# Two-layer attention and recurrence: order of the denominators' sums, and later slots for some projections

## The chip, the cores and the metric

The kernel runs on one NeuronCore of a Trainium2 chip. The metric is the device time of one execution in microseconds. Before the change three runs took 2109.12, 2111.13 and 2114.09 us (median 2111.13).

## What is computed

The input `x` has four batches of 128 channels and 64 x 64 positions, so N = 4096 positions (tokens) per batch, in float32. Two layers follow each other:

```python
# layer 0: attention over all positions, 64 inner channels
att = softmax(einsum('bmi,bmj->bij', wk @ x, wq @ x), axis=2)
x   = x + wo @ (att applied to wv @ x)

# layer 1: token layout t = x^T
t = t + causal_attention(_ln_t(t), Wq, Wk, Wv)        # 128 channels, scale 128**-0.5
t = t + ffn(_ln_t(t), W, V, gamma, beta)
# ffn: Wx = batchnorm(_ln_t(t) @ W^T), then over time
#      y_t = sigmoid(Wx_t + y_{t-1} @ V^T)
```

## The kernel before

`fast_path` does the work (another path, taken when a range flag is set, did not run). All of `x` stays in SBUF as `xs`. A batch has NB = 8 blocks of 512 query positions per layer. The kernel runs batch by batch: the eight blocks of layer 0, then the eight of layer 1.

**Items and slots.** Each block is cut into items of two key tiles (128 keys each) against the 512 queries: 16 items for a block of layer 0, 2g + 2 items for block g of the causal layer 1. The main loop (L923) gives every item a slot `s`. In slot `s` TensorE forms the scores of item `s` (`scores`, L791 in layer 0, L800 in layer 1) into PSUM `s_ps` (two buffers), ScalarE takes the exponential into `p` (L805, L807; four buffers), VectorE (DVE) adds `p` into `dsum` (`sums`, L831 and L839), and TensorE multiplies the `p` of item `s - 2` with the values into `acc` (`values`, L851 and L859). A `p` buffer is free again when both the values and the sum have read it.

**Block's end.** With the last item of a block, `values` copies `acc` to SBUF (`half` L870 and the add L871 in layer 0, `agg` L873 in layer 1), and DVE adds the two halves of `dsum` into `den` (L875). What remains for the block is a chain of small tasks, which the loop runs in later slots, one due task per slot at most, the earliest due first; slots without one go to the `side` list (the next batch's keys and values).

- `folded` (L561) sums `den` over partitions: a 32 x 32 block transpose (L565) and a reduction (L567) leave `part`, four quarters per token. Either TensorE sums and spreads them (`by_pe`, L573, with a DVE multiply L574), or five DMAs on the SP queue carry them through DRAM (four L579, then L580). The result is `own`.
- `project` (L583) sums the quarters of `own` (L586), inverts the sum (L587), multiplies `agg` with the output matrix in four matmuls into `o_ps` (L590) and adds the scaled result to `xs` in four DVE instructions (L595, called STTs below).
- `normed` (L599) is the layer norm of the block: statistics, a power on GpSimd (POOL, L458), a few short DVE steps (L459 to L462) and four scalings (L611).
- Layer 0 continues with `by_channels` (L655): a DVE transpose and eight SP DMAs (L659, L664) that form `xhT`. Layer 1 (`finish1`, L683) writes the block to `x2` (L701), forms its own `xhT` with a DVE transpose and five SP DMAs (`second`, L719 and L723), and multiplies it with the recurrence's input matrix (`third`, L727), with statistics on DVE (L730) and a copy into `xs` on ScalarE (L740).

In layer 0 the projection is not tied to a slot: `first` (L672) folds and puts `second` on the list `fill`, and the main loop takes one entry from `fill` at the end of the next block (L938). In layer 1 the numbers of `yield` (L750 to L756) say how many slots after the task before a task is due: `first` two slots after `sums`, `second` three after `first`, `third` four after `second` (six for the blocks folded on TensorE, g < 2).

**Who sets the order.** Slots give the order in which instructions are written. The tile framework then orders each engine's queue by a simulated time of its own, with the written order as priority, so an instruction whose inputs it takes to be ready may be put ahead of others written earlier. `tc.keep_in_program_order(ins)` adds an edge from the instruction last written for the same engine to `ins`; it is an order in the queue and no semaphore. After the last block the recurrence over time and the output follow.

Of the kernel before, what the change touches and what calls it, by code (L numbers as in the profile page):

```python
# [11 lines left out]
ALU = mybir.AluOpType  # L12
AX = mybir.AxisListType
# [336 lines left out]
def fast_path(  # L350
# [21 lines left out]
    nc = tc.nc  # L372
# [4 lines left out]
    NB = N // BLK  # L377
# [86 lines left out]
    with tc.tile_pool(name="batch", bufs=1) as batch, tc.tile_pool(name="rows", bufs=2) as rowp, tc.tile_pool(  # L464
# [7 lines left out]
        def misc(name):  # L472
            return ps_m.tile([P, BLK], F32, tag="m", name=name)
# [109 lines left out]
        def project(layer, b, g, agg, own):  # L583

            rec = recs[:, layer, b, ts(g, TPB)]
            nc.vector.tensor_reduce(rec, own.rearrange("p q j -> p j q"), AX.X, ALU.add)  # L586
            nc.vector.reciprocal(rec, rec)  # L587
            op = misc("o_ps")
            for j in range(TPB):
                nc.tensor.matmul(  # L590
                    op[:, ts(j, P)], lhsT=agg[:, ts(j, P)], rhs=wv1 if layer else wo2, start=True, stop=True
                )
            for j in range(TPB):
                t = xs[:, b, ds(g * BLK + j * P, P)]
                nc.vector.scalar_tensor_tensor(  # L595
                    t, in0=op[:, ts(j, P)], scalar=rec[:, j : j + 1], in1=t, op0=ALU.mult, op1=ALU.add
                )

        def normed(b, g, dst):  # L599

            st = stat.tile([P, TPB, nc.vector.BN_STATS_DIM], F32, tag="st", name="ln_st")
            mv = stat.tile([P, TPB, nc.vector.BN_AGGR_DIM], F32, tag="mv", name="ln_mv")
            for j in range(TPB):
                nc.vector.bn_stats(st[:, j], xs[:, b, ds(g * BLK + j * P, P)])  # L604
                nc.vector.bn_aggr(mv[:, j], st[:, j])
            var = stat.tile([P, TPB], F32, tag="var", name="ln_var")
            nc.vector.tensor_scalar(var, mv[:, :, 1], LN_EPS, None, ALU.add)  # L607
            y = stat.tile([P, TPB], F32, tag="rstd", name="ln_rstd")
            rsqrt(y, var, stat.tile([P, TPB], F32, tag="z", name="ln_z"))
            for j in range(TPB):  # L610
                nc.vector.tensor_scalar(  # L611
                    dst[:, j], xs[:, b, ds(g * BLK + j * P, P)], mv[:, j, 0:1], y[:, j : j + 1], ALU.subtract, ALU.mult
                )

        def transposed(src, dst, name, engine):

            ps = misc(name)
            for j in range(TPB):
                nc.tensor.transpose(ps[:, ts(j, P)], src[:, j], ident)
            engine(dst, ps)  # L620

        def squares(src):

            sq = wk.tile([P, Q, TPB, S], F32, tag="sqT", name="sqT")
            nc.vector.transpose(out=sq.rearrange("p c j t -> p j c t"), in_=src.rearrange("p j (c r) -> p j c r", r=S))
            return sq

        def in_range(last):

            r = recs.rearrange("p l b t -> p (l b t)")  # L630
            r = r[:, -TPB:] if last else r[:, :-TPB]
            r2 = wk.tile([P, BLK], F32, tag="den", name="r2")[:, : r.shape[-1]]
            nc.vector.tensor_scalar(r2, r, LOW, None, ALU.is_ge)
            nc.vector.tensor_scalar(r, r, HIGH, None, ALU.is_le)
            nc.vector.tensor_tensor(r, r, r2, ALU.mult)
            nc.vector.tensor_reduce(good[:, 1:2] if last else good[:, 0:1], r, AX.X, ALU.add)
# [46 lines left out]
        def finish1(b, g):  # L683
            agg, den = bs[b].agg, bs[b].den
            mem = {}
            final = b == B - 1 and g == NB - 1

            def warm(n, rhs):

                ps = ps_s.tile([P, 2 * BLK], F32, tag="s", name="warm_ps")  # L690
                for _ in range(n):
                    nc.tensor.matmul(ps[:, : BLK // 2].rearrange("p (a c) -> p a c", c=P) if len(rhs.shape) == 3 else ps[:, : BLK // 2], lhsT=ident, rhs=rhs, start=True, stop=True)

            def first():
                if final:

                    nc.scalar.activation(spare, agg[:, 0:1], AF.Sigmoid)
                project(1, b, g, agg, mem["own"])
                if final:
                    warm(9, agg[:, : BLK // 2])  # L700
                nc.sync.dma_start(  # L701
                    out=x2[b, ts(g, BLK)].rearrange("(j p) c -> p j c", p=P),
                    in_=xs[:, b, ts(g, BLK)].rearrange("p (j c) -> p j c", c=P),
                )
                mem["xh"] = wk.tile([P, TPB, P], F32, tag="xh2", name="xh2")
                normed(b, g, mem["xh"])

            def second():
                mem["xhT"] = wk.tile([P, BLK], F32, tag="xhT2", name="xhT2")
                if final:  # L710
                    transposed(mem["xh"], mem["xhT"], "xh2T_ps", nc.vector.tensor_copy)
                    warm(1, mem["xh"][:, 2:])
                    return


                sq = squares(mem["xh"])
                by_c = dram2.tile([Q, S, Q, P], F32, tag="by_c", name="by_c")
                for q in range(Q):
                    nc.sync.dma_start(  # L719
                        out=by_c[:, :, q].rearrange("c r k -> r c k"),  # L720
                        in_=sq[ts(q, S)].rearrange("r c j t -> r c (j t)"),
                    )
                nc.sync.dma_start(out=mem["xhT"], in_=by_c.rearrange("c r q k -> (c r) (q k)"))  # L723

            def third():
                wp = misc("wx_ps")
                nc.tensor.matmul(wp, lhsT=wf, rhs=mem["xhT"], start=True, stop=True)  # L727
                if b == B - 1 and g == NB - 1:
                    in_range(True)
                nc.vector.bn_stats(ends[:, 3:] if final else stats[:, b * NB + g], wp)  # L730
                if b == B - 1 and g == NB - 2:
                    ahead()
                    in_range(False)

                to = xs[:, b, ts(g, BLK)]
                if final:
                    nc.scalar.copy(to.rearrange("p (s c) -> p s c", c=CPB), wp.rearrange("p (c s) -> p s c", s=STEPS))
                    warm(6, to[:, : BLK // 2])
                else:
                    nc.scalar.copy(  # L740
                        to.rearrange("p (s j q u) -> p s j q u", q=Q, j=TPB, s=STEPS),
                        wp.rearrange("p (q j u s) -> p s j q u", q=Q, j=TPB, s=STEPS),
                    )

            by_pe = final or g < 2

            def sums():
                mem["own"] = folded(den, by_pe)

            if by_pe:  # L750
                yield 1, lambda: (sums(), first())
            else:
                yield 1, sums
                yield 2, first
            yield 3, second
            yield 1 if final else 6 if g < 2 else 4, third  # L756


        class Item:
# [118 lines left out]
        fill = []  # L878
# [44 lines left out]
        for s in range(len(items) + SKEW + 16):  # L923
            if s < len(items):
                it = items[s]
                if it.first:
                    bs[it.b].rows = bs[it.b].next.pop(0)
                    if it.layer and it.g == 1 and it.b + 1 < B:
                        for m in range(NB // 2):
                            side += keys(it.b + 1, m)  # L930
                scores(it)
            if 0 <= s - SKEW < len(items):
                it = items[s - SKEW]
                values(it)
                if it.last:
                    rows()
                    tokens()
                    if fill:  # L938
                        fill.pop(0)(s)
                    push(s, (finish1 if it.layer else finish0)(it.b, it.g))  # L940
            if s < len(items):
                sums(items[s])
            due = [w for w in waiting if w[0] <= s]
            if due:
                w = min(due, key=lambda w: w[0])
                waiting.remove(w)
                w[1]()
                push(s, w[2])
            elif side:
                side.pop(0)()  # L950
                if not side and items[s].b == 0 and items[s].layer == 0:
                    tokens()
                    load_rest()
                    form_half()
# [165 lines left out]
```

## Time and profile before

| engine | busy us | share of the span | instructions |
|---|---|---|---|
| TensorE matmul | 2068.2 | 98% | 11764 |
| VectorE (DVE) | 1489.1 | 70% | 2853 |
| ScalarE (ACT) | 1007.1 | 48% | 1095 |
| GpSimd (POOL) | 117.9 | 6% | 221 |

The span of the profiled execution is 2112.6 us. The share of busy time is an average; TensorE's matmuls overlap, and a busy TensorE can be one at a lower clock. A slot of layer 0 takes 1.72 us where nothing waits (from one exponential L805 to the next). The transfer of `own` takes 1.5 to 3.0 us from issue to landing, 1.7 at the median. In the lists of waits, `A <- B: x, n, m` says that A's engine stood idle until B was done, x us in all, n times, m at the longest; in the timeline a line has the start, the duration, the engine, the line of the kernel, the operation and, in brackets, the idle time before it with what ended it.

### The profile page before, as it was taken

What the parts mean: (1) busy time and instruction counts of PE and PEld (TensorE: products, weight loads), DVE (VectorE), ACT (ScalarE), POOL (GpSimd) and SP (SyncE); (2) the same over time, 40 slices, a digit from 0 to 9 for tenths busy, and PEclk for the clock granted to TensorE, in tenths of its full rate; (3) what the DMA queues carried; (4) which work ended last, traced back from release to release, by engine and by line L of the source; (5) the groups of instructions that cost most, each with busy time, mean ns of one, the idle gap of its engine ahead of it and who ended that gap; (6) DMA issues with size and microseconds to landing.
All of it is one profiled execution on the core that took longest, in us unless ns stands there. A gap on an engine that the chain in (4) does not pass through costs nothing. (4 is left out here: it accounts for less than half of the span.)

```text
span 2112.6 us, 30728 instructions
## 1 busy us (share of the span) xinstructions
PE 2068.2 (98%) x11764; PEld 902.4 (43%) x11764; DVE 1489.1 (70%) x2853; ACT 1007.1 (48%) x1095; POOL 117.9 (6%) x221
## 2 busy tenths in 40 slices
PE   9999999999999999999999999999999999999998
PEld 3333354444333344444333335444433334544466
DVE  4888875545788896454688888544478988755568
ACT  5666633333665643333466653333356664333355
POOL 1000010000000011000000001000000001100000
PEclk9999999999999999999999999999999999999999
DMA  3110122100110112110011012110000111200044
GB/s 111 52 22 12 21 66 61 31 16 16 56 22 13 20 36 70 45 31 16 16 52 16 17 21 66 53 38 16 15 17 12 22 22 26 51 21 26 16 164 161
DMA packets 179499, 82.71 MB, mean 39 GB/s; under 512 B 114849, under 2 KB 163489, under 8 KB 178321
## 3 DMA queue, kind: packets, MB, share of 16 engines
q1 hardware_dynamic: 178336, 80.12, 14.4%
q8 instruction: 94, 1.54, 0.3%
q14 instruction: 61, 0.49, 0.1%
q0 software_dynamic: 288, 0.39, 0.1%
q10 hardware_dynamic: 720, 0.16, 0.0%
HBM read 42.69 MB, written 33.74 MB: 36 GB/s over the span
## 5 line engine op out<-in xcount | busy, mean ns | idle before, releaser
L831 DVE TENSOR_TENSOR dsum<-dsum,p 128x1024 f32<-128x1024 f32 x676 | 825.6, 1221 | 376.0 <-ACT p L807 292.4
L805 ACT ACTIVATE p<-s_ps,nshift 128x1024 f32<-128x1024 f32 x512 | 571.1, 1116 | 353.2 <-PE s_ps L791 271.8
L791 PE MATMUL s_ps<-kr 64*64 64x512 f32 x2048 | 530.6, 595 | 16.7 <-ACT p L805 16.7
L807 ACT ACTIVATE p<-s_ps 128x1024 f32<-128x1024 f32 (+2 forms) x288 | 274.2, 952 | 551.8 <-PE s_ps L800 521.0
L851 PE MATMUL acc<-p,v 64*64 64x512 f32 x4096 | 534.0, 592 | 1.7 <-ACT half L870 1.7
L791 PE MATMUL s_ps<-swap,kr 64*64 64x512 f32 x2048 | 530.6, 595 | 4.3 <-ACT p L805 4.3
L800 PE MATMUL s_ps<-rows,xhT 128*128 128x512 f32 (+3 forms) x1152 | 502.9, 559 | 0.0
L859 PE MATMUL acc<-p,xh 128*128 128x512 f32 (+3 forms) x1152 | 500.8, 557 | 0.0
L859 PEld LDWEIGHTS acc<-p,xh 128*128 128x128 f32 x1152 | 216.2, 190 | 244.3 <-issue 233.8
L800 PEld LDWEIGHTS s_ps<-rows,xhT 128*128 128x128 f32 x1152 | 213.4, 190 | 241.9 <-issue 208.4
L851 PEld LDWEIGHTS acc<-p,v 64*64 64x64 f32 x4096 | 155.3, 133 | 286.1 <-issue 272.7
L791 PEld LDWEIGHTS s_ps<-kr 64*64 64x64 f32 x2048 | 138.0, 133 | 157.5 <-issue 118.0
L791 PEld LDWEIGHTS s_ps<-swap,kr 64*64 64x64 f32 x2048 | 138.0, 133 | 143.6 <-issue 126.1
L458 POOL TENSOR_TENSOR ln_rstd<-ln_var,mhalf 128x4 f32<-128x4 f32 x64 | 69.7, 1090 | 1175.2 <-DVE ln_var L607 1147.6
L839 DVE TENSOR_TENSOR dsum<-dsum,p 128x256 f32<-128x256 f32 (+1 forms) x120 | 55.8, 498 | 58.0 <-POOL p L811 58.0
L595 DVE SCALAR_TENSOR_TENSOR xs<-o_ps,recs,xs 128x128 f32<-128x128 f32 x256 | 73.6, 344 | 7.0 <-PE o_ps L590 6.1
L611 DVE TENSOR_SCALAR xh<-xs,ln_mv,ln_rstd 128x128 f32<-128x128 f32 x256 | 71.7, 342 | 2.3
L811 POOL TENSOR_SCALAR_AFFINE_SELECT p<-p 128x128 f32<-128x128 f32 x128 | 40.4, 339 | 551.7 <-ACT p L807 546.0
L604 DVE BATCH_NORM_STATS2 ln_st<-xs 128x6 f32<-128x128 f32 x256 | 63.6, 270 | 0.0
L740 ACT COPY xs<-wx_ps 128x512 f32<-128x512 f32 x31 | 18.1, 585 | 85.7 <-DVE stats L730 85.7
L459 DVE TENSOR_TENSOR ln_z<-ln_rstd 128x4 f32<-128x4 f32 x64 | 10.5, 164 | 67.5 <-POOL ln_rstd L458 67.5
L829 DVE COPY dsum<-p 128x1024 f32<-128x1024 f32 x60 | 41.1, 684 | 18.7 <-ACT p L807 15.5
(137 smaller groups left out, 1046.7 us busy)
## 6 DMA issues: line engine op xcount, KB each, us to landing
xs<-in_xT SPq DMA_DIRECT2D x32, 256.0 KB, 3.1
by_r<-sqT SPq DMA_DIRECT2D x128, 64.0 KB, 2.2
xhT<-by_r SPq DMA_DIRECT2D x128, 64.0 KB, 2.0
x<-xs SPq DMA_DIRECT2D x32, 256.0 KB, 2.3
xr<-x SPq DMA_DIRECT2D x8, 1024.0 KB, 12.4
out_x<-xr SPq DMA_DIRECT2D x16, 512.0 KB, 5.1
by_c<-sqT SPq DMA_DIRECT2D x124, 64.0 KB, 1.8
xhT<-by_c SPq DMA_DIRECT2D x31, 256.0 KB, 2.6
```

The costliest lines, as they stand in the source:

```text
L458: nc.gpsimd.tensor_tensor(y, var, mhalf[:, : y.shape[-1]], ALU.pow)
L595: nc.vector.scalar_tensor_tensor(t, in0=op[:, ts(j, P)], scalar=rec[:, j : j + 1], in1=t, op0=ALU.mult, op1=ALU.add)
L604: nc.vector.bn_stats(st[:, j], xs[:, b, ds(g * BLK + j * P, P)])
L611: nc.vector.tensor_scalar(dst[:, j], xs[:, b, ds(g * BLK + j * P, P)], mv[:, j, 0:1], y[:, j : j + 1], ALU.subtract, ALU.mult)
L791: nc.tensor.matmul(ps[c * M : c * M + M, off : off + n], lhsT=bs[it.b].kr[part, h, ds(t % (NT // 2) * P + c * M, M)], rhs=rows[h], start=True,
L800: nc.tensor.matmul(ps[:, off : off + n], lhsT=lhsT, rhs=rhs, start=True, stop=True)
L805: nc.scalar.activation(it.p[:, :off], ps[:, :off], AF.Exp, bias=nshift)
L807: nc.scalar.activation(it.p[:, :off], ps[:, :off], AF.Exp, scale=float(P) ** -0.5)
L831: nc.vector.tensor_tensor(flat, flat, it.p, ALU.add)
L839: nc.vector.tensor_tensor(den[:, h, q0:], den[:, h, q0:], it.p[:, o : o + n], ALU.add)
L851: nc.tensor.matmul(bt.acc[h * M : h * M + M, r], lhsT=bt.v[part, t], rhs=it.p[part, o : o + n], start=it.first, stop=it.last,)
L859: nc.tensor.matmul(bt.acc[:, 0, q0:], lhsT=bt.xh[:, t], rhs=it.p[:, o : o + n], start=it.first and h == 0, stop=it.last and h == 1,)
```

## The change

Four edits in three places:

- The sum over the quarters (L586) is pinned: it is put behind the DVE instruction that was written before it. It serves both layers and all 64 blocks.
- In layer 1, for blocks whose denominators go through DRAM (g >= 2, except the very last block of the last batch), `first` is due three slots after `sums`, not two.
- In layer 1, for the last block (g = 7) of batches 0 to 2, `third` is due six slots after `second`, not four.
- The main loop takes nothing from `fill` at the end of block 0 of layer 1.

```diff
         def project(layer, b, g, agg, own):
 
             rec = recs[:, layer, b, ts(g, TPB)]
-            nc.vector.tensor_reduce(rec, own.rearrange("p q j -> p j q"), AX.X, ALU.add)
+
+            tc.keep_in_program_order(nc.vector.tensor_reduce(rec, own.rearrange("p q j -> p j q"), AX.X, ALU.add))
             nc.vector.reciprocal(rec, rec)
...
             else:
                 yield 1, sums
-                yield 2, first
+                yield 3, first
             yield 3, second
-            yield 1 if final else 6 if g < 2 else 4, third
+            yield 1 if final else 6 if g < 2 or g == NB - 1 else 4, third
...
                 if it.last:
                     rows()
                     tokens()
-                    if fill:
+
+                    if fill and (it.layer == 0 or it.g):
                         fill.pop(0)(s)
                     push(s, (finish1 if it.layer else finish0)(it.b, it.g))
```

## The prediction

> **What bounds the kernel now.** I read the busy times first, then who waits for whom on TensorE, ScalarE and VectorE, then the order of time around the waits that TensorE suffers.
>
> ```profile
> PE 2068.2 (98%) x11764; PEld 902.4 (43%) x11764; DVE 1489.1 (70%) x2853; ACT 1007.1 (48%) x1095; POOL 117.9 (6%) x221
> ```
>
> TensorE has an instruction in flight for 2068.2 of 2112.6 us, so the change, which removes no matmul, can win only from the other 44 us, or from matmuls that run slowly. Waits, as total us, times, longest:
>
> ```profile
> PE s_ps L791 <- ACT p L805: 21.0, 23, 2.7
> PE wx_ps L727 <- DMA xhT<-by_c: 6.3, 3, 3.2
> ...
> ACT p L805 <- DVE dsum L831: 67.8, 69, 4.1
> ...
> DVE ln_z L459 <- POOL ln_rstd L458: 67.5, 64, 1.2
> DVE recs L586 <- DMA own<-by_token: 40.9, 30, 3.7
> ```
>
> Two waits hold 27.3 us. The first is a chain: layer-0 scores find no free PSUM because the exponential (L805) has not run; it finds no free `p` buffer because DVE has not yet added an old `p` into `dsum` (L831); and DVE is behind after a block's end, where the fold, projection and norm fall together. One such end, in order of time (start, duration):
>
> ```profile
> 639.82 0.69 DVE L875 TENSOR_TENSOR den<-dsum 128x512 f32<-128x512 f32 x1
> ...
> 643.82 0.34 DVE L595 SCALAR_TENSOR_TENSOR xs<-o_ps,recs,xs 128x128 f32<-128x128 f32 x1
> ...
> 644.68 0.86 DVE L595 SCALAR_TENSOR_TENSOR xs<-o_ps,recs,xs 128x128 f32<-128x128 f32 x3
> 646.20 0.34 SPq L580 DMA_DIRECT2D own<-by_token  x1
> 646.37 0.16 DVE L605 BATCH_NORM_AGGREGATE ln_mv<-ln_st 128x2 f32<-128x6 f32 x1
> 649.00 0.18 DVE L586 TENSOR_REDUCE recs<-own 128x4 f32<-128x16 f32 x1 [2.46 <-DMA own<-by_token]
> 649.10 1.22 DVE L831 TENSOR_TENSOR dsum<-dsum,p 128x1024 f32<-128x1024 f32 x1
> 654.32 6.50 DVE L831 TENSOR_TENSOR dsum<-dsum,p 128x1024 f32<-128x1024 f32 x5
> 655.60 1.11 ACT L805 ACTIVATE p<-s_ps,nshift 128x1024 f32<-128x1024 f32 x1 [4.07 <-DVE dsum L831]
> 656.77 0.94 PE L791 MATMUL s_ps<-swap,kr 64*64 64x512 f32 x2
> ...
> 1552.46 2.05 PE L727 MATMUL wx_ps<-xhT,wf 128*128 128x512 f32 x2 [3.21 <-DMA xhT<-by_c]
> ```
>
> The reader is to see that L586 at 649.00 belongs to the block that ended at 641, and its result is used at the next end, some 30 us later: the STTs (L595) at 644.68 serve the block before. The scheduler has pulled it forward into the busiest stretch of DVE, where it stands 2.46 us for its transfer, with the `dsum` behind it. The last line is the second wait: layer 1's last block of a batch asks for `xhT` before it lands.
>
> Slow matmuls show in the stretches (length, busy PE, PEld, DVE, ACT, POOL, clock, DMA):
>
> ```profile
> 1546.00:1549.00 3.00, 3.00 (x32) 0.91 (x24) 2.79 (x3) 1.80 (x3) 0.00 (x0) 1.00 0.30 71
> 1552.50:1556.00 3.50, 3.50 (x10) 0.98 (x14) 0.70 (x1) 0.59 (x1) 0.00 (x0) 0.50 0.00 0
> ```
>
> After the 3.21 us wait the granted clock is 0.50 for the next stretch; so a long wait costs more than its listed length.
>
> **What the Trainium skill says.** "TensorE: Matmul & The Clock Gate", section Part 1 on the HAM clock gate, has the array fall to half clock after an idle window of about 3.4 us; the trace agrees with 0.50 after 3.21 us. The same page, under the architectural detail of the array, calls ScalarE's and VectorE's queues strictly in order; the trace agrees, DVE starting nothing between 646.37 and 649.00. "DMA: Bandwidth & Descriptors", Rules for kernel authors, advises issuing a transfer early and waiting for it late; this trace shows the opposite at L586.
>
> **The pin.** It adds no instruction and no semaphore, only an order on DVE: each sum over the quarters goes behind whatever DVE instruction was written before it. In layer 0 that is the next block's `den` (L875), so reduce and reciprocal (0.174 + 0.165 us by their rows) leave their own block's end and join the next one's. Each end loses one pair and gains one, so the work there is unchanged; what goes is the wait. By then `own` landed long ago (about 25 us). Behind the pair stand the STTs, which need its result and already start 4 us after `den` (643.82 against 639.82 above), so 0.34 us in front of them is free within that burst. For the nine blocks folded on TensorE the instruction before is the multiply that feeds the sum (L574): nothing moves.
>
> What it is worth I take from the blocks that happened not to wait. Interval between successive `half` copies (L870) shows a block's length; the three with a projection inside and no TensorE wait, from 81.85, 674.36 and 1087.03, last 28.71 or 28.72 us. For blocks 1 to 5 of each batch, DVE's wait at L586, then excess over 28.71: batch 0: 0/0, 0.64/0.79, 0.18/1.04, 0.40/0.89, 0.25/0.73; batch 1: 0.96/0.59, 0/0.53, 2.46/4.66, 0/0.01, 1.09/1.24; batch 2: 0/0, 1.18/1.38, 1.08/1.58, 0.88/1.37, 0.92/1.41; batch 3: 1.55/1.19, 0.79/1.28, 0/0.47, 0/0.60, 0/0.40. The excesses sum to 20.16. The seven blocks with zero wait average 2.01/7 = 0.29. If all twenty become like these, 20.16 - 20 x 0.29 = 14.4 us go. Block 6 has DVE waits of 2.19, 2.60, 2.95, 2.03 and TensorE waits of 1.50, 1.69, 2.03, 1.34 (6.56 in all); each DVE wait exceeds the TensorE wait, so all of it should go, with about 0.24 us beside each (124.16: listed wait 0.55, excess 0.79): 7.5 us. Block 0's waits (2.11, 1.97, 1.95, 3.68) cost TensorE nothing: no projection follows a layer-0 start, and these blocks all last 28.12. Sum for the pin: 21.9 us.
>
> In layer 1 the sum falls behind the current slot's `dsum`, itself waiting for the exponential. TensorE's scores, values and projection of that slot end about together with that `dsum` (1033.83 for the STT against 1032.69 + 1.22 for the `dsum`), so at most 0.4 us are added before the STTs; layer 1's block lengths repeat to 0.02 us over batches 0 to 2 and show no wait to make longer.
>
> **Projection one slot later (23 blocks, g >= 2).** Moved: reduce, reciprocal, four projection matmuls, four STTs, the 256 KB write L701, then the norm with its POOL power (1.09 us), and with it the five DMAs of L719 and L723. A layer-0 slot is 1.72 us, a layer-1 slot about 3.2. On SP these go past nothing due: the next L579 comes with the next block's end. On POOL the next masks (L811) come at the end of a block of eight items or more. Price nothing; TensorE's other matmuls hide it. The DVE waits that it removes in layer 1 (0.4 to 2.1 us each) stand beside a busy TensorE: gain nothing.
>
> **Recurrence inputs two further slots later (last block, batches 0 to 2).** From the projection, TensorE now reaches L727 after seven slots plus the projection, 13.3 us (1047.13 - 1.53 - 1032.27). `xhT` lands after 14.88, 14.86 and 16.55 us. Two more slots make 16.76. With 0.4 us of delay from the pin the landings are 15.3, 15.3, 16.95: a wait of 0.2 at worst. From the end of the block to its copy after, intervals are 31.74, 31.73, 36.17; the last carries the halved clock. Without waits each is 30.2: savings 1.5 + 1.5 + 6.0 = 9.0 us. It still falls in the same 16-slot block (slot 13). Moved are one matmul, the statistics (0.69), and a copy (0.58).
>
> **The condition on `fill`.** It does nothing, as I read the slots. After layer 0's last block the norm of the block before takes slot 1, so its own fold runs in slot 2, after that slot has asked `fill`; layer 1's block 0 ends in just that slot and finds it empty. The trace agrees: the projection with `wo` comes at 284.26, beside the copy of layer 1's block 1 (283.87), none at 268.99. Price 0, gain 0.
>
> **Sum.** 21.9 + 9.0 = 30.9, less about 0.5 for the late pair and the tight third transfer: 30 us. The profiled span 2112.6 becomes 2082. That execution took 2114.27; the other runs 2109.12 to 2114.09, median 2111.13, so 2111 - 30 = 2081.
>
> **Rivals.** Half (18%): the scheduler lays out the emptied DVE differently, and part of the lag stays, made of the burst itself and of the 1.1 us wait for POOL in each norm. Half the pin's gain and all of the other is 11 + 9 = 20, giving 2091. For it: zero-wait blocks still lose up to 0.60. Against: excess follows the wait over thirteen blocks (mean wait 0.95, mean excess 1.40).
>
> No effect (4%): the edge doesn't hold the sum back, or the freed time turns into another wait of equal size; 2111. Against: blocks at 28.71 exist.
>
> Slower (8%): the pair in front of the fold makes the scheduler put one of the two `dsum` adds inside the burst (649.10, 1.22 us) after the norm's chain. TensorE then waits 1.22 + 0.24 us more in each of 24 bursts, 35 us: 2111 - 31 + 35 = 2115. It decides from 31/24 = 1.3 us per burst. For it: order on DVE is the scheduler's, and 4 `p` buffers are little reserve. Against: the pair (0.34) is little over a quarter of such an add.
>
> **How the numbers follow.** The forecast (70%) has its own range 2074 to 2089: the low end if the zero-wait blocks' 5.7 us go as well (36.6 saved), the high end with 22 saved. Range for 8 in 10: 2074 to 2096, which takes in most of the half case. A change under 0.2% (4 us) cannot be told from none. Faster 0.70 + 0.18 = 0.88; within 0.04; slower 0.08.
>
> **What would show it.** Waits of L586 on DMA near zero in layer 0 (40.9 now); L791's 21.0 down to 3 to 6; L727's 6.3 under 1; ScalarE's 67.8 on `dsum` about halved; `half` intervals of blocks 1 to 5 between 28.7 and 29.3; no 0.50 clock near 1550. Wrong, if L791's waits remain while L586's are gone: then the burst, not the transfer, made DVE late.

## The result and the profile after

The changed kernel takes 2079.07 us at the median of five runs (2078.65 to 2080.69), the kernel before 2111.13; the ratio is 0.9847, 95% interval 0.9833 to 0.986. The profiled execution spans 2078.9 us against 2112.6, so 33.7 us are to be explained. Every ratio is to the kernel before on the same chip. Lines of the kernel after L585 have moved by one: the pinned sum is L587, the layer-0 scores L792, the exponential L806, the sum over `p` L832, the recurrence's input matmul L728. Runs whose edit adds lines move them further.

Busy times, from the page of the changed kernel:

```profile
PE 2058.7 (99%) x11764; PEld 900.9 (43%) x11764; DVE 1481.6 (71%) x2853; ACT 1007.1 (48%) x1095; POOL 117.0 (6%) x221
```

Who waits for whom on TensorE, ScalarE and VectorE:

```profile
PE acc L852 <- ACT half L871: 1.9, 4, 0.5
PE s_ps L792 <- ACT p L806: 1.8, 3, 0.6
...
ACT p L806 <- DVE dsum L832: 49.9, 68, 2.0
...
DVE ln_z L459 <- POOL ln_rstd L458: 68.1, 64, 1.2
```

The scores' 21.0 us are 1.8. The recurrence input's 6.3 us of waiting for a transfer and DVE's 40.9 us of waiting for `own` are gone from the lists altogether. TensorE's busy time fell too, by 9.5 us at the same number of matmuls. 5.0 us of that lie in blocks 1 to 6 of layer 0, 2.0 between layer 1's last block and the next batch, the rest at the start and the end: a matmul after a wait takes longer, and after long waits the clock was lower for some us. One of these waits was in the block's end that the prediction shows: TensorE stood for 2.72 us until 656.77, and in the stretch behind it the kernel before had a granted clock of 0.50 (the third figure from the end):

```profile
657.00:660.00 3.00, 3.00 (x16) 0.80 (x12) 2.79 (x3) 2.15 (x2) 0.00 (x0) 0.50 0.32 58
```

This is why that block lost 4.66 us for a wait of DVE of 2.46. In the changed kernel, a block's end in the same batch and place as that one, in order of time:

```profile
633.00 0.69 DVE L876 TENSOR_TENSOR den<-dsum 128x512 f32<-128x512 f32 x1
633.62 0.17 DVE L587 TENSOR_REDUCE recs<-own 128x4 f32<-128x16 f32 x1
...
637.01 0.34 DVE L596 SCALAR_TENSOR_TENSOR xs<-o_ps,recs,xs 128x128 f32<-128x128 f32 x1
...
638.99 0.34 SPq L580 DMA_DIRECT2D own<-by_token  x1
...
639.64 1.19 DVE L832 TENSOR_TENSOR dsum<-dsum,p 128x1024 f32<-128x1024 f32 x1
...
644.83 5.17 DVE L832 TENSOR_TENSOR dsum<-dsum,p 128x1024 f32<-128x1024 f32 x4
...
646.11 1.11 ACT L806 ACTIVATE p<-s_ps,nshift 128x1024 f32<-128x1024 f32 x1 [1.69 <-DVE dsum L832]
```

L587 now stands directly behind `den`. It serves the block before, whose `own` landed long ago; the `own` of the block that just ended is sent for only 5.4 us later (638.99). The burst of work from `den` through the fold and the norm no longer stops for a transfer, and keeps only its wait of 1.12 us for POOL; ScalarE waits 1.69 us for a `p` where it waited 4.07, and TensorE no longer stops.

Block lengths (from one copy of the accumulator to the next, with the number of the copy that begins the stretch) place the 33.7 us. 28.71 us is the length of a layer-0 block in which nothing waits, and the excess is what a block takes beyond it. The third row is called the turn below.

| stretch | before | after | gain |
|---|---|---|---|
| layer 0, blocks 1 to 5, excess over 28.71, all batches | 20.16 | 2.45 | 17.7 |
| layer 0, block 6, four times | 130.26 | 122.29 | 8.0 |
| from layer 1's last block into the next batch, three times | 99.64 | 93.15 | 6.5 |
| start, to the first copy | 53.73 | 53.50 | 0.2 |
| end, from the last copy | 92.5 | 91.2 | 1.3 |

Layer 1's block lengths sum to the same as before. The first three rows come to 32.2 us, and the medians differ by 32.1. The end is not the change's: with the very same instruction order another execution ended in 89.5 us (the run without the condition on `fill`, below).

### The profile page after: what moved, and what is told of

Read it like the earlier page. It is cut to its first block, busy times and chain, and to the rows that moved or that the text cites. A ratio compares the mean times of both kernels' runs of the same rounds, so it can differ in the third digit from the quotient of the medians.

```text
span 2078.9 us, 30768 instructions
## 1 busy us (share of the span) xinstructions
PE 2058.7 (99%) x11764; PEld 900.9 (43%) x11764; DVE 1481.6 (71%) x2853; ACT 1007.1 (48%) x1095; POOL 117.0 (6%) x221
## 3 DMA queue, kind: packets, MB, share of 16 engines
q8 instruction: 94, 1.54, 0.3%
## 4 chain that ended last, share of the span: by engine, by line
PE 81%; DVE 15%; issue 2%; ACT 1%; POOL 1%; DMA 0%; DVEq 0%; ACTq 0%; POOLq 0%
PE s_ps L801 22%; PE acc L860 22%; PE s_ps L792 14%; PE acc L852 13%; DVE dsum L832 9%; PE y_ps L1017 2%; PE o_ps L591 2%; PE r_ps L556 1%; PE wx_ps L728 1%; PE kr_ps L513 1%; ACT p L806 1%; PE v_ps L525 1%; DVE xr L1038 1%; POOL ln_rstd L458 1%; DVE xs L596 1%
## 5 line engine op out<-in xcount | busy, mean ns | idle before, releaser
L832 DVE TENSOR_TENSOR dsum<-dsum,p 128x1024 f32<-128x1024 f32 x676 | 825.3, 1221 | 401.4 <-ACT p L808 310.7
L806 ACT ACTIVATE p<-s_ps,nshift 128x1024 f32<-128x1024 f32 x512 | 571.2, 1116 | 325.2 <-PE s_ps L792 269.5
L792 PE MATMUL s_ps<-swap,kr 64*64 64x512 f32 x2048 | 528.2, 592 | 2.9 <-ACT p L806 1.8
L792 PE MATMUL s_ps<-kr 64*64 64x512 f32 x2048 | 528.2, 592 | 0.4
L792 PEld LDWEIGHTS s_ps<-swap,kr 64*64 64x64 f32 x2048 | 138.4, 133 | 139.7 <-issue 123.7
L792 PEld LDWEIGHTS s_ps<-kr 64*64 64x64 f32 x2048 | 138.5, 133 | 138.0 <-issue 120.9
```

What stands on the lines that cost most here:

```text
L792: nc.tensor.matmul(ps[c * M : c * M + M, off : off + n], lhsT=bs[it.b].kr[part, h, ds(t % (NT // 2) * P + c * M, M)], rhs=rows[h], start=True,
L806: nc.scalar.activation(it.p[:, :off], ps[:, :off], AF.Exp, bias=nshift)
L832: nc.vector.tensor_tensor(flat, flat, it.p, ALU.add)
```

## Experiments

**One part at a time.** The pin without the later slots (the kernel before, with):

```diff
-            nc.vector.tensor_reduce(rec, own.rearrange("p q j -> p j q"), AX.X, ALU.add)
+            tc.keep_in_program_order(nc.vector.tensor_reduce(rec, own.rearrange("p q j -> p j q"), AX.X, ALU.add))
```

> The kernel before with the pin alone (first still two slots after sums, third four after second, fill unconditioned). Theory (the hoisted sum's wait for its transfer makes DVE late in layer 0, and the two parts add): layer 0 gains what it gained with the whole change, about 26 us in the block intervals, while the waits of the recurrence's input matmul (about 6 us listed, 6 to 9 with the slow clock after them) stay: 2083 to 2089 us, and DVE's wait for own under 3 us in layer 0. Rival (the gain comes from the later slots): 2100 to 2111.

Measured: 2086.12 us (2085.81 to 2087.41), ratio 0.9874 [0.9859, 0.9889], 26.6 us faster. Blocks 1 to 5 keep 2.49 us of excess and block 6 sums to 122.31, as with the whole change: 17.7 + 8.0 = 25.6 us of gain in layer 0 come from the pin alone. DVE waits nowhere for `own`. The recurrence's input still waits:

```profile
PE wx_ps L727 <- DMA xhT<-by_c: 7.3, 3, 3.4
```

The later slots without the pin (the changed kernel, with the diff above reversed):

> The changed kernel without the pin (later slots kept). Theory: only the waits of the recurrence's input matmul go, 5 to 9 us: 2102 to 2106, with DVE's wait for own still 25 us or more and the layer-0 score waits still near 20 us. Rival (later slots are what frees DVE): 2080 to 2090.

Measured: 2108.68 us (2106.37 to 2112.18) beside 2112.86 for the kernel before on that chip, ratio 0.9982 [0.9975, 0.9989]: about 4 us, less than expected. The recurrence's wait is gone and the three intervals fall from 99.64 to 92.01. But the unpinned sums wait as before, and in this execution layer 0 pays a little more for it: 23.28 in blocks 1 to 5 (20.16 before) and 131.26 in block 6 (130.26).

```profile
PE s_ps L792 <- ACT p L806: 25.6, 25, 2.6
...
DVE recs L587 <- DMA own<-by_token: 41.9, 32, 3.8
```

So about five sixths of the gain are the pin's, and the slots do not free DVE.

**The slots and the condition, each undone in the changed kernel.** `third` at four slots:

```diff
-            yield 1 if final else 6 if g < 2 or g == NB - 1 else 4, third
+            yield 1 if final else 6 if g < 2 else 4, third
```

> The changed kernel with third four slots after second again in the last block of each batch. Theory: TensorE asks for the recurrence's input 13.3 us after the projection again, xhT lands 14.5 us or more after it, so waits of 1 to 3 us come back in three places, 4 to 9 us in all: 2083 to 2088. Rival (the order on SP or DVE in the changed kernel already brings xhT sooner): 2078 to 2081.

Measured: 2088.95 us (2087.95 to 2089.84), ratio 0.9901 [0.9884, 0.9917], a little beyond the expected range. The waits return, and the three intervals rise from 93.15 to 102.70, by 9.6 us for 7.3 us of listed wait, although the changed kernel's 1.8 us of waiting for `p` (all of it at the turns) are gone here:

```profile
PE wx_ps L728 <- DMA xhT<-by_c: 7.3, 3, 3.4
```

In this run one of the waits was 2.00 us (it ended at 539.95). The stretches around it (length, busy time and count of PE, PEld, DVE, ACT, POOL, then the granted clock, DMA share, GB/s):

```profile
537.00:540.00 3.00, 1.00 (x13) 0.15 (x5) 2.79 (x3) 1.11 (x1) 0.00 (x0) 1.00 0.29 87
540.00:543.00 3.00, 3.00 (x10) 0.77 (x14) 2.20 (x3) 0.59 (x1) 0.00 (x0) 0.57 0.00 0
543.00:546.00 3.00, 3.00 (x28) 0.96 (x24) 1.23 (x1) 1.55 (x2) 0.00 (x0) 0.87 0.03 5
```

The clock is at 0.57 for the 3 us after the wait. It fell behind the other two waits of this run as well (0.62 over 3 us after 1.92 us, 0.50 after 3.43). That is where more time is lost than the list shows.

`first` at two slots:

```diff
-                yield 3, first
+                yield 2, first
```

> The changed kernel with first two slots after sums again. Theory (the slot of the projection in layer 1 stands beside a busy TensorE): no change, 2077 to 2081; DVE's wait for own comes back with a few us in layer 1. Rival (it holds DVE at the start of the next batch's layer 0 or keeps PSUM longer): 2083 or more.

Measured: 2078.75 us (2078.51 to 2081.78), ratio 0.9856 [0.984, 0.9873]: no difference from the change. DVE waits nowhere for `own` even so; my side remark that a few us would come back was wrong.

The condition on `fill` removed:

```diff
-                    if fill and (it.layer == 0 or it.g):
+                    if fill:
```

> The changed kernel without the condition on fill. Theory (the list is empty at the end of layer 1's first block): the order of every engine is that of the changed kernel, the time is the same, 2078 to 2081. Rival (it puts off the projection of layer 0's last block): another order and another time. The run also shows how far two runs of one instruction order lie apart.

Measured: 2078.95 us (2078.43 to 2081.8), ratio 0.9857 [0.9841, 0.9874]. The instruction order on every engine is that of the changed kernel, so the condition does nothing. The profiled span was 2076.7 against 2078.9: two executions of one order differ by 2 us.

The pin in layer 0 alone (here and below `...` within a line stands for arguments left out):

```diff
-            tc.keep_in_program_order(nc.vector.tensor_reduce(rec, ..., AX.X, ALU.add))
+            total = nc.vector.tensor_reduce(rec, ..., AX.X, ALU.add)
+            if layer == 0:
+                tc.keep_in_program_order(total)
```

> The changed kernel with the pin in layer 0 alone; in layer 1 the scheduler places the sum. Theory (the pin's whole effect is in layer 0): the same time as the change, 2077 to 2082. Rival (part of the gain comes from the order in layer 1): 2085 or more.

Measured: 2080.57 us (2077.66 to 2081.22), ratio 0.9852 [0.9834, 0.987]: the same time. The sums of layer 1 wait 3.1 us again, in five places, and TensorE doesn't notice. The trace shows that the pin in layer 1 even costs a little: the three turns take 30.55 to 30.56 us each, where they take 31.05 with it. These 1.5 us are too few to show in the times, the more so as blocks 1 to 5 lose 0.7 us more in this execution.

**Why a DVE wait costs TensorE so directly.** The kernel before, with a fifth `p` buffer:

```diff
-        name="prob", bufs=4
+        name="prob", bufs=5
```

> The kernel before with five p buffers in place of four and nothing else; TensorE's and ScalarE's order is that of before. Theory (the wait costs time only because no p buffer is free when DVE is late): the waits of DVE for own stay near 40 us, but a fifth buffer lets ScalarE run one item (1.72 us) further ahead, so that layer-0 score waits fall from 21 to under 5 us; with the recurrence waits untouched 2083 to 2092. Rival (DVE's wait holds TensorE through something else, such as the projection's PSUM): 2105 to 2112.

Measured: 2102.61 us (2100.73 to 2104.89), ratio 0.9956 [0.9942, 0.9969]. Neither theory: some 9 us, where I expected 20 to 29.

```profile
PE s_ps L791 <- ACT p L805: 17.2, 19, 1.7
...
DVE recs L586 <- DMA own<-by_token: 46.1, 30, 3.8
```

The block lengths say why. Excess over 28.71 in blocks 1 to 5: batch 0: 0.01, 0.00, 0.30, 1.35, 0.85; batch 1: 0.01, 0.01, 1.46, 1.54, 1.95; batch 2: 0.01, 1.57, 0.78, 0.60, 0.46; batch 3: 0.01, 1.20, 0.51, 0.45, 0.53. The first blocks are now clean, and the later ones still lose. The sum falls from 20.16 to 13.60, between 0.9 and 2.3 us in a batch and 1.64 on average, about the one slot (1.72 us) that a buffer can hold. (The profiled execution gains elsewhere too: its third turn takes 31.75 us, where the kernel before had 36.17 with the halved clock, and its end is 3.0 us shorter.) So the buffer only stores a lead, which DVE then doesn't win back. A stretch of one layer-0 block of the changed kernel without a TensorE wait, and all that DVE waits for in two of them (663.2 to 721.18):

```profile
663.20:692.18 28.98, 28.95 (x266) 10.56 (x266) 26.26 (x45) 18.77 (x18) 1.01 (x1) 1.00 0.12 20
...
DVE ln_z L459 <- POOL ln_rstd L458: 2.2, 2, 1.1
```

DVE is busy for 26.26 of 28.98 us (91%, against 71% over the span) and waits only 1.1 us per block, for POOL; the other 1.6 us lie between its 45 instructions. Successive `den` show its own period:

```profile
662.00 0.69 DVE L876 TENSOR_TENSOR den<-dsum 128x512 f32<-128x512 f32 x1
...
691.00 0.69 DVE L876 TENSOR_TENSOR den<-dsum 128x512 f32<-128x512 f32 x1
```

That is 29.00 us, in nearly every one of these blocks, and TensorE's is 28.71: a layer-0 block with a projection is 0.29 us longer for DVE than for TensorE. The lead that pays for this can be read too. In batch 1 `den` starts 2.04 us before the accumulator is copied at the end of block 0, then 1.76, 1.48 and 1.20, and from there on about 1.18: three blocks cost TensorE nothing, and the following ones lose 0.27 to 0.29. With five buffers in the kernel before, the lead shrinks until `den` starts 0.54 us after the copy, 1.72 us or one slot further. The new theory: in layer 0 DVE is at its limit, and any time added to its queue lengthens the block once the stored lead is gone.

Two extra adds per block in the changed kernel test the first half of it. They write a tile `scratch` that nothing reads (its declaration is left out here):

```diff
             tc.keep_in_program_order(nc.vector.tensor_reduce(rec, ..., AX.X, ALU.add))
+            if layer == 0:
+                for _ in range(2):
+                    tc.keep_in_program_order(nc.vector.tensor_tensor(scratch, agg, agg, ALU.add))
```

> The changed kernel with two extra adds of 128x512 into a scratch tile (about 0.69 us each) pinned behind each layer-0 sum: 1.4 us more of DVE at each end of a layer-0 block. Theory (any DVE time at a block's end counts, waiting or working, beyond a small reserve): in blocks 1 to 6 of each batch TensorE loses 1.0 to 1.7 us more, 24 to 40 us in all: 2103 to 2119. Rival (only the wait for the transfer did harm, DVE has reserve at 71% busy): under 5 us, 2079 to 2084.

Measured: 2100.24 us (2098.21 to 2101.91), ratio 0.9939 [0.9925, 0.9952], 19 to 21 us slower than the change: below the theory's range, far above the rival's.

```profile
PE s_ps L796 <- ACT p L810: 18.0, 20, 1.3
```

Block 1 of each batch loses 0.31 to 0.44, most of the later ones 1.16 to 1.18, where the change has at most 0.29. The 1.17 is DVE's period again:

```profile
670.08 0.69 DVE L880 TENSOR_TENSOR den<-dsum 128x512 f32<-128x512 f32 x1
...
699.95 0.69 DVE L880 TENSOR_TENSOR den<-dsum 128x512 f32<-128x512 f32 x1
```

29.87 us less 28.71 is 1.16. The two adds last 0.68 us each, but lengthen the period by 0.87 us only, 29.87 against 29.00: the instructions beside them do not depend on them and follow each other more closely than without them. I had counted 1.4 us. Block 6, which runs into layer 1, loses only 0.26 more; I had counted it in full.

The second half, a lead that is spent once, got its number before the run. The same extra time (two reductions of 128x512 with one column out) with five `p` buffers:

```diff
-                    tc.keep_in_program_order(nc.vector.tensor_tensor(scratch, agg, agg, ALU.add))
+                    tc.keep_in_program_order(nc.vector.tensor_reduce(scratch, agg, AX.X, ALU.add))
...
-        name="prob", bufs=4
+        name="prob", bufs=5
```

> The changed kernel with two extra reductions of 128x512 behind each layer-0 sum (as long as the extra adds of the run before, 0.68 us each; the output is one column) and five p buffers. It tells what limits a layer-0 block when DVE has more to do. Theory (DVE is then the engine that a block waits for, and a buffer only stores lead): the fifth buffer is used up once in each batch, about 1.7 us, so blocks 1 to 5 lose 21.2 - 4 x 1.7 = 14 us in all over their 28.71, with the loss small in blocks 1 and 2 and about 1.2 in 4 and 5: 2091 to 2097. Rival (too few p buffers is the limit, DVE has time): the loss is under 4 us: 2078 to 2084.

Measured: 2096.02 us (2095.64 to 2099.31), ratio 0.9942 [0.9929, 0.9955]. Batch 0 loses 0.01, 0.00, 0.97, 1.15, 1.50 in blocks 1 to 5, the others follow the same course, and the sum is 14.00 us, as forecast from DVE's limit. Ratios of the run with two extra adds and four buffers (0.9939) and of this one hardly differ: of the 7 us gained in these blocks, 4.7 are lost in a new place, the stretch behind layer 1's first copy, with 3.8 us of listed wait:

```profile
PE kr_ps L514 <- DVE xs L600: 3.8, 3, 1.5
```

There the next batch's projection finds its PSUM held by a late DVE.

**Towards a faster version.** `third` at five slots in the last block:

```diff
-            yield 1 if final else 6 if g < 2 or g == NB - 1 else 4, third
+            yield 1 if final else 6 if g < 2 else 5 if g == NB - 1 else 4, third
```

> The changed kernel with third five slots after second in the last block (six in the change, four before). Theory: in the changed kernel the copy of the recurrence's input stands right before the end of layer 0's first block and costs TensorE 0.60 us and a restart each of three times; one slot earlier it doesn't, and xhT (about 14.6 us after the projection, TensorE asks after 15.0) has landed: 1 to 2.5 us faster than the change, 2076 to 2078. Rival: xhT lands late in one batch and the wait comes back, 2079 to 2082.

Measured: 2080.4 us (2080.33 to 2082.76), ratio 0.9863 [0.9847, 0.9879]: nothing gained, as the rival had it. The transfer's waits come back, and the scores' wait that I meant to remove stays in two of three places:

```profile
PE wx_ps L728 <- DMA xhT<-by_c: 2.2, 3, 1.6
...
PE s_ps L792 <- ACT p L806: 1.3, 2, 0.7
```

With a fifth `p` buffer besides:

> The changed kernel with third five slots after second in the last block and with five p buffers. Theory: the fifth buffer takes what DVE's lag still costs in layer 0 (0.3 us in some eight blocks, 2.5 us) and the earlier slot the 0.6 us at three ends: 2073 to 2077. Rival (what is left in layer 0 is not for want of p): as with third five alone, 2076 to 2079.

Measured: 2077.98 us (2077.57 to 2081.81), ratio 0.9848 [0.9829, 0.9867]. This is the rival's range. Layer 0's blocks are clean (0.1 us of excess in all, 2.45 in the change), as the theory had it, but the waits at the turns stay. The best combination takes the pin in layer 0 alone, the change's slots and five buffers:

> The pin in layer 0 alone, the change's slots, and five p buffers. Theory: layer-0 blocks fall to 28.71 us as with five p buffers before (2.5 us less than the change) and the interval behind the recurrence's input stays at 30.55 as with the pin in layer 0 alone (1.5 us less): 2074 to 2078, the fastest of all, though hardly apart from the change. Rival: 2079 or more.

Measured: 2075.73 us (2075.3 to 2077.84), ratio 0.9843 [0.983, 0.9857]. Excess 0.1 us, three turns of 30.55 us (31.05 in the change). Its interval overlaps the change's, so by timing they are not told apart; the traces show 2.4 and 1.5 us less at these two places.

## Why the prediction held

The forecast was 2081 us with a range from 2074 to 2096; 2079.07 was measured. The cause was the one named, but that the sum came within 2 us is in part luck: the pin gave 3.8 us more than forecast and the recurrence's input 2.5 us less. By its steps:

- **The pin, 21.9 us: right in kind, short by 3.8.** Alone and within the change it gave 25.6 to 25.7. Block 6 came out as worked out (7.5 forecast, 8.0 found). The term that was mis-sized is the rest left in blocks 1 to 5: the average of the seven blocks without a wait, 0.29, was taken for all twenty, 5.7 us; 2.45 stay. That average mixed two kinds of block. DVE's period was 29.1 to 29.3 us in all seven, but three began with the full lead of 2.04 us and lost at most 0.01, and four began with it used up (1.17 to 1.18 us) and lost 0.40 to 0.60, which is the period less 28.71. In the changed kernel DVE's period is 29.00, and only the last two blocks of each batch pay its 0.29. Why the period is 0.1 to 0.3 us shorter than in those seven was not looked into.
- **That the work at a block's end is unchanged: right.** The sum and the reciprocal sit behind `den` as foreseen, the STTs still start 4.0 us after `den` (637.01 against 633.00), and the `dsum` add stayed inside the burst (639.64), which was what the slower rival doubted.
- **The recurrence's input, 9.0 us: 6.5 within the change.** The wait went in all three places, also the tight one. What the sum missed is a new wait of the scores just ahead of the next copy. With the later slots alone it is 0.10 us in two of the three places and the turn takes 30.55 us, where 30.2 was assumed; the pin in layer 1 makes it 0.60 and the turn 31.05, as the run with the pin in layer 0 alone shows. That late pair was priced together with the tight transfer at 0.5 us in all; it costs 1.5. Without the two extra slots the changed kernel loses 9.6 us in those places, so what the waits cost was about what was taken for them.
- **First one slot later: nothing, as said.** Undoing it leaves the time where it is.
- **The condition on `fill`: nothing, as said.** The order of every engine is the same without it.
- **Not forecast:** 1.3 us at the end and 0.2 at the start. Two executions of the same order already differ by 1.7 us at the end and 0.4 at the start, so nothing shows that these are the change's.
- **A sign that did not come:** ScalarE's 67.8 us of waiting for `dsum` were to be about halved; 49.9 stay. They hardly hold TensorE, whose scores wait 1.8 us for `p` in all.

Among the rivals, "half" fell because the lag did not remain. What the prediction did not know is why the transfer's wait passed to TensorE. It spoke of little reserve in `p` buffers; the runs with five buffers showed that the buffers only store a lead and that DVE itself is at its limit in layer 0. Of DVE's 40.9 us of waiting for `own`, 22.1 stood in blocks 1 to 6 of layer 0, and only these counted; with the restarts and the lower clock behind TensorE's waits, 25.7 us were won there. The 9.7 us in block 0, which has no projection and lasts 28.12 us before and after, and the 9.0 in layer 1 cost nothing. The skill's advice to wait late for a transfer ("DMA: Bandwidth & Descriptors", Rules for kernel authors) is borne out for an engine that has no time left. Its remark on the half clock after about 3.4 us of idleness ("TensorE: Matmul & The Clock Gate", Part 1) does not fit these traces as well as the prediction says: 3.21 us is already less, and a lower clock was met after much shorter waits, 0.68 over 3 us after one of 1.89 us.

## What to carry to other kernels

A wait in an engine's in-order queue is priced by the stage, not by the span: list the engine's busy time and waits for one period of the stage, and if they fill it, every wait there lengthens the period. The same wait where the engine has time costs nothing, as in block 0. Periods that happen to lack the wait are a good forecast of its removal, but look at the lead with which each begins, and take the saturated engine's own period rather than an average. Here a deeper buffer in front of a saturated engine paid once per batch, not once per block.

## What was not expected of the hardware

- In the 3 us after a wait, the granted TensorE clock was 0.57 after 2.00 us (`third` at four slots) and 0.50 after 2.72 us (before). In the pin-only run it was 0.68 after a wait of 1.89 us, but stayed at 1.00 after one of 2.03. After 1.66 us (five buffers) and less it was 1.00 where looked at. The turn with the 1.89 us wait took 33.79 us, the one with the 2.03 us wait 32.23. So here a wait of some 1.9 us or more could cost about twice its listed length, but need not.
- Two DVE instructions of 0.68 us placed among independent ones took 0.60 and 0.57 us until the next one started (640.90 to 641.50 and 642.18 to 642.75), and lengthened DVE's period by 0.87 us together.
